# Outputs' tiles in their own pool over the stored rows, the first unit filled like the later ones, and a finished half's projection at earlier places

## The chip, the cores and the metric

The kernel runs on one core of one Trainium2 chip. The metric is device time in microseconds (us) of one launch; lower is better. TensorE is called PE, VectorE DVE, ScalarE ACT, GpSimd POOL and SyncE SP, as in the profile.

## The reference

A model of two layers on x of shape (B=2, T=1024, E=256), all in float32. Every block is followed by a residual add and a layernorm over E.

```python
x = layernorm(x + attn0(x))   # causal grouped-query attention: 32 q heads, 8 kv heads, D=8, rope, softmax
x = layernorm(x + ffn0(x))    # silu(x Wg * sg) * (x Wu * su), then Wd * sd; int8 weights, FF=1024
x = layernorm(x + attn1(x))   # gated delta rule, below
x = layernorm(x + ffn1(x))    # relu(x sign(Wu)^T * s) sign(Wd)^T * s, FF=1024

# attn1: 16 heads, key and value width 128
q, k, v = silu(conv4(x Wq)), silu(conv4(x Wk)), silu(conv4(x Wv))   # causal depthwise conv over 4 tokens
a, b = sigmoid(x Wa + ba), sigmoid(x Wb + bb)                       # per token and head
for t:                                                              # per batch and head; k scaled by 128**-0.5
    S = a_t * S - b_t * (S k_t - v_t) k_t^T
    o_t = S q_t
o = layernorm_per_head(o) * ln_w + ln_b
return (o * sigmoid(x Wg)) Wo
```

## The kernel before

Products that need float32 accuracy are split in a high and a low part and done as three matmuls each (`mm3`, L968 to L970).

**Order.** Layer 0 (attention, then FFN in blocks of two token tiles of 128, 16 tiles in all) ends at about 803 us of the span. Then comes the delta rule (`delta_rule`), as 32 *units*. `place(i)` gives unit i as (hi, s): hi is one of four halves of 512 tokens, s one of eight pairs of heads. A unit has two heads and four chunks of 128 tokens. So units 7, 15, 23 and 31 (s == NS - 1) are the last ones of a half: with them a half's rows are complete.

PE's order in the delta rule is written by hand: each piece of work is a generator that yields the place of its next step, each unit has 120 places (`UNIT`), and `lines.add(generator, at, base)` puts it in. On PE instructions keep this order strictly (`te.link`, `te.strict`). On the other engines and on SP's queue of DMA issues the framework's scheduler decides the order, and each engine then works its queue in order.

Pieces of a unit i:

- `recur(i)`, the chain over four chunks c: `pr` (place 30c; L673 and L677, transposed v plus k times the state M), copied by ACT to `prs` (L680); `pw` (30c+10, L688), copied to `wc` (L691); then `pm` (L700) and `po` (L715, L716) at 30c+20. DVE makes the next state M (L705 from no state, L707 else), ACT copies po to `o` (L719), DVE takes its moments (`ost`, `om`, L657, L658).
- `others(i+1)`: v projection of the next unit (place 1), q (31), key rows, gate (61), gate rows, scores `pkq` (71, 81). The projections' convolutions are four taps (L275) on DVE, `far` and `halos` (L289, L272) on ACT, adds (L292) on POOL.
- `keys(i+4)` (AHEAD = 4): k projection at AT_KEYS = 91, decay scans (L325) on DVE at 113, triangles (L339) from 131.
- `decayed`: POOL multiplies k and q by the decay rows `dg` (L519, L521), which a DMA on SP's queue loads.
- `blocks` (even i; a chain of small DVE steps on `pi` and `tmp`, L384 and L390) and `levels` (odd i; L420 `p`, L423 `n` on DVE, L431 `px`), which build the inverse of the triangles.
- `finish(i)`, which runs inside unit i+1 at the four places AT_FINISH: normalises o with a reciprocal root `om` (`rsqrt`: L931 to L933 on DVE, then twelve small steps on POOL, L940 to L943, then L599 on DVE; the eight tiles of o are then normalised by POOL, DVE and ACT in turn, L606 and L609), transposes it (`pt`, L615, two heads at the first two places), multiplies with the gate `gt` (`y`, L619), splits y in `yh` and `yl` (POOL, L623 and L917), and at the last two places projects with Wo (`pf`, 12 matmuls each, L633) and adds to the residual rows `xtok` (L636). For s == NS - 1 a layernorm of these rows follows each of the two adds: bn statistics (L948, L949), `rsqrt` on DVE (L931 to L938, on the tile `ln`), scaling (L952). After both, the half is stored (`store_tokens`, L927).

Before unit 0, `rest_of_first` sets up what the first unit needs: decays and decayed k, q of unit 0, then the v and q projections of unit 1, and the k projection and convolution of unit 4. In later units these stand inside the unit before.

**Pools.** At the start of the delta rule the SBUF of layer 0's rows (`x`, pool `toks`) and of its FFN is free again. `open_late` opens over it one pool ("late") for the tiles of the recurrence (prs, wc, M, o, om, ost) and of the output (gt, xtok, wo, y, yh, yl), and one ("w") for weights and decay rows.

**Layer 0's last steps.** Each FFN block ends with `layernorm(..., eng=nc.gpsimd)` on two token tiles (three rounds of a root step: twelve steps on POOL, or nine on DVE where `eng` is None) and a store of those rows. The last block's layernorm runs while unit 1's projections have begun.

The line numbers are those of the kernel before.

Of the kernel before, what the change touches and what calls it, by code (L numbers as in the profile page):

```python
# [12 lines left out]
F32R = mybir.dt.float32r  # L13
# [7 lines left out]
P = 128  # L21
# [10 lines left out]
HP = 2  # L32
# [56 lines left out]
AT_LEVELS = 43, 53, 73, 83, 103, 113, 132, 142  # L89
AT_FFN = 24  # L90
AT_FINISH, AT_FINISH_LAST, AT_HALF = (41, 51, 101, 111), (31, 41, 71, 76), ((22, 30, 46), (1, 6, 13))

FFN0, FFN1, FFN1_LAST, FFN1_TAIL = 7.6, 22.0, 27.0, 40.0

# [50 lines left out]
def delta_rule(  # L145
# [23 lines left out]
    ps_m = open_pool(left, "ps_m", "left", 2, PSUM)  # L169

    def open_late():
        pools["late"] = open_pool(right, "dlate", "right", 2)
        pools["w"] = open_pool(outer, "dw", "right")
        for name, bufs in (("c", 2), ("t", 1), ("l", 1)):
            pools[name] = open_pool(right, "ps_" + name, "right", bufs, PSUM)
# [6 lines left out]
    def half_tile(pool, tag, bufs):  # L182
        return pool.tile([P, HT], F32, name=tag, tag=tag, bufs=bufs)
# [297 lines left out]
    def pair(m, i):  # L481

        pps = [project(m, i, h) for h in range(HP)]
        for h in range(HP):
            conv(m, i, h, pps[h])
        if i < last:
            yield AT_OUT
        for h in range(HP):
            conv_out(m, i, h, pps[h])
# [35 lines left out]

    def gate_rows(i):
        for h in range(HP):
            g = half_tile(pools["late"], "gt", 5)
            made = nc.scalar.activation(g, st[i]["pg"][h], AF.Tanh, scale=0.5)
            if copied:  # L530
                after(made, copied[-1])
            st[i]["gt", h] = g
# [25 lines left out]
    def rest_of_first():  # L558
        decays(0)
        for which in "kq":  # L560
            for h in range(HP):
                decayed(0, h, which)
        te.strict, te.last = True, ended[0]
        for m in "vq":
            drain(pair(m, 1))
        ks = keys(AHEAD, AT_KEYS)
        next(ks)
        lines.add(ks, next(ks), 0)

    def gate_of_first():  # L570
        gate(0)
        yield GAP
        gate_rows(0)

    def finish(i, o, m, chunks, places):

        hi, s = place(i)
        if s == 0:
            halves[hi]["x"] = load_tokens(pools["late"], hi * HC, HC)
        x = halves[hi]["x"]  # L580
        if chunks[0] == 0:
            st[i]["wo"] = []
            for part in range(2):
                t = pools["late"].tile([P, HP, E], F32R, name=f"wo{part}", tag=f"wo{part}", bufs=1)
                nc.sync.dma_start(
                    out=t.bitcast(F32),
                    in_=w1d["o", part][s * HP * P : (s + 1) * HP * P, :].rearrange("(h p) e -> p h e", p=P),
                )
                st[i]["wo"].append(t)
        wo = st[i]["wo"]  # L590
        c1, nc_ = chunks[0], len(chunks)
        final = i == last and chunks[-1] == HC - 1
        slow = None if i == last else nc.gpsimd
        ahead = tc.high_priority if final else nullcontext
        t1 = slice(c1 * P, (c1 + nc_) * P)
        rs, nb = m[:, :, 2], m[:, :, 3]
        with ahead():
            rsqrt(rs, m[:, :, 1], m[:, :, 4], m[:, :, 5], EPS * SCALE * SCALE, slow)
            nc.vector.scalar_tensor_tensor(nb, m[:, :, 0], -1.0, rs, ALU.mult, ALU.mult)  # L599
            for c in chunks:  # L600
                for h in range(HP):
                    n = (c - c1) * HP + h
                    oc, r1 = o[:, c, h, :], rs[:, n : n + 1]
                    how = (NORM if i < last else NORM_LAST)[n]
                    if how == "A":
                        nc.scalar.activation(oc, oc, AF.Identity, bias=nb[:, n : n + 1], scale=r1)  # L606
                    else:
                        eng = nc.gpsimd if how == "P" else nc.vector
                        eng.tensor_scalar(oc, oc, m[:, n, 0:1], r1, ALU.subtract, ALU.mult)  # L609
        ys = []  # L610
        for h in range(HP):
            yield places[h]
            pt = bank(pools["t"], "t", "pt")[:, 0 : nc_ * P]
            for c in chunks:
                te.link(nc.tensor.transpose(pt[:, (c - c1) * P : (c - c1 + 1) * P], o[:, c, h, :], ident))  # L615
            y = half_tile(pools["late"], "y", 1)[:, 0 : nc_ * P]
            with tc.high_priority():
                nc.scalar.activation(pt, pt, AF.Identity, bias=lnb, scale=lnw)
                nc.vector.scalar_tensor_tensor(y, st[i]["gt", h][:, t1], 1.0, pt, ALU.add, ALU.mult)  # L619
            yh = pools["late"].tile([P, HT], F32R, name="yh", tag="yh", bufs=2)[:, 0 : nc_ * P]  # L620
            yl = pools["late"].tile([P, HT], F32R, name="yl", tag="yl", bufs=2)[:, 0 : nc_ * P]
            with ahead():
                (nc.gpsimd.tensor_copy if i < last else nc.scalar.copy)(yh, y)  # L623
                sub_low(nc.gpsimd if i < last else nc.vector, yl, y, yh)
            ys.append((yh, yl))
        for c0 in range(0, nc_, 2):
            yield places[2 + c0 // 2]
            pf = bank(pools["t"], "t", "pf").rearrange("p (c e) -> p c e", e=E)
            for c in range(2):
                for h in range(HP):  # L630
                    t = slice((c0 + c) * P, (c0 + c + 1) * P)
                    yh, yl = ys[h]
                    mm3(pf[:, c, :], yh[:, t], yl[:, t], wo[0][:, h, :], wo[1][:, h, :], h == 0, h == HP - 1)  # L633
            xc = x[:, c1 + c0 : c1 + c0 + 2, :]
            with ahead():
                nc.vector.tensor_add(xc, pf, xc)  # L636
                if s == NS - 1:
                    layernorm(gx, x, c1 + c0, 2, eng=nc.gpsimd if i == last and not final else None)
            if s == NS - 1:
                halves[hi]["done"] = c1 + c0 + 2  # L640
        if s == NS - 1 and hi < 2 * B - 1:
            store_tokens(xs, hi * HC, x)

    def recur(i):
# [8 lines left out]
        def moments(c):  # L653
            for h in range(HP):
                st6 = pools["late"].tile([P, 6], F32, name="ost", tag="ost")
                with tc.high_priority() if i == last and c == HC - 1 else nullcontext():
                    nc.vector.bn_stats(st6, o[:, c, h, :])  # L657
                    nc.vector.bn_aggr(m[:, c * HP + h, 0:2], st6)  # L658
            part = HC // 2 if i == last else HC
            if c % part == part - 1:  # L660
                chunks = range(c + 1 - part, c + 1)
                at = i * UNIT + 3 * GAP * (c + 1) + 3
                lines.add(finish(
                    i, o, m[:, chunks[0] * HP : (c + 1) * HP, :], chunks,
                    AT_HALF[c // part] if i == last else AT_FINISH_LAST if i == last - 1 else AT_FINISH,
                ), at, at if i == last else (i + 1) * UNIT)

        for c in range(HC):
# [172 lines left out]
    def drain(g):  # L841
        for _ in g:
            pass

    for i in range(-AHEAD, last + 1):
# [9 lines left out]
            open_late()  # L855
        if i < -1:
            lines.add(keys(i + AHEAD, 0), t)
        elif i > 0 and i + AHEAD <= last:
            lines.add(keys(i + AHEAD, AT_KEYS), t + AT_KEYS, t)
        if i == -2:  # L860
            lines.add(others(0), t)
# [3 lines left out]
        elif 0 <= i < last:  # L865
            lines.add(others(i + 1), t + AT_ROWS, t)
        if i == 0:
            lines.add(gate_of_first(), t + AT_QUERIES)
        if i >= 0:
            lines.add(recur(i), t, chain=True)  # L870
# [27 lines left out]
def tile_two_layers(ctx: ExitStack, tc: tile.TileContext, a, out):  # L898
# [22 lines left out]
    def load_tokens(pool, n, count, bufs=1, tag="xtok"):  # L921
        t = pool.tile([P, count, E], F32, name="xtok", tag=tag, bufs=bufs)
        nc.sync.dma_start(out=t, in_=xs[n * P : (n + count) * P, :].rearrange("(n p) e -> p n e", p=P))
        return t
# [91 lines left out]
    def open_pool(group, name, side, bufs=1, space=bass.MemoryType.SB):  # L1016
        return group.enter_context(tc.tile_pool(name=name, bufs=bufs, side=side, space=space))
# [467 lines left out]
    def open_ffn(group):  # L1485
# [20 lines left out]
        def block(n):  # L1506
# [45 lines left out]
            with tc.high_priority() if n == NT - 2 else nullcontext():  # L1552
                for i in range(2):
                    y = new("fy", [P, E], 2)
                    nc.vector.tensor_mul(y, po[i], s_down)
                    nc.vector.tensor_add(x[:, n + i, :], y, x[:, n + i, :])
                anchor["norm"] = layernorm(pool, x, n, 2, eng=nc.gpsimd)
                store_tokens(xs, n, x[:, n : n + 2, :])
            yield 0.2

# [127 lines left out]
```

## Time and profile before

| | |
|---|---|
| median of 3 runs | 2052.26 us (2052.05 to 2056.88) |
| profiled execution | 2052.92 us, of it span 2051.20 us, 1.72 us around it |
| mean granted TensorE clock | 0.977 |
| PE busy | 1888.1 us |
| DVE, ACT, POOL busy | 1475.0, 1266.7, 1077.4 us |
| delta rule, from the first prs copy | at 821.0 us of the span |
| units 0, 1, 2, 3 (from prs to prs) | 26.2, 37.1, 31.3, 38.9 us |
| units 8, 9; 16, 17; 24, 25 | 33.5, 43.4; 30.9, 49.7; 33.5, 40.1 us |
| PE idle within units 9, 17, 25 | 5.6, 9.5, 3.5 us |

Busy PE time is time with a matmul on the array; the granted clock is the share of full speed at which it ran. The length of a unit is the time between the first copies (prs, L680) of two successive units. Even units of a batch's first half have less to do than odd units, which also carry `levels`; units are therefore compared with others of the same parity. In an answer of waits a row reads: engine and line, what it waited for, us in total, times, longest.

### The profile page before, as it was taken

The numbers are of one execution on the slowest core, as the hardware profiler recorded it, in microseconds if no ns is written. First come the engines' busy times: TensorE is split into PE (matmuls) and PEld (weight loads), VectorE is DVE, ScalarE is ACT, GpSimd is POOL, SyncE is SP. The second block draws the span as 40 slices with busy tenths as digits, with TensorE's granted clock in tenths as the row PEclk, the third lists the DMA queues.
The fourth block names the chain that finished last, engine by engine and source line by source line (L and its number), as shares of the span: only waits on it lengthen the run. The fifth ranks groups of instructions, "written<-read, shape, count | busy, mean of one in ns | idle before, by whom it ended". The sixth has DMA issues, their size and how long they took to land.

```text
span 2051.2 us, 49222 instructions
## 1 busy us (share of the span) xinstructions
PE 1888.1 (92%) x18657; PEld 1491.8 (73%) x18657; DVE 1475.0 (72%) x3477; ACT 1266.7 (62%) x2731; POOL 1077.4 (53%) x1739
## 2 busy tenths in 40 slices
PE   5898889999998898999999899999899999999986
PEld 3454455555556787888889789888888888888775
DVE  5756666887756995676787787678678679766566
ACT  1365556566655366567676676776676766676542
POOL 4353333331124464666776656666567676665453
PEclk8999999999999999899999999999999999999997
DMA  5564443441232431443444434345434344443010
GB/s 169 165 190 133 147 131 125 149 135 55 69 77 62 116 92 55 134 123 110 127 115 116 142 99 118 115 115 137 116 101 133 114 126 109 125 135 96 18 52 22
DMA packets 312998, 229.17 MB, mean 112 GB/s; under 512 B 139640, under 2 KB 278904, under 8 KB 312760
## 3 DMA queue, kind: packets, MB, share of 16 engines
q1 hardware_dynamic: 299640, 210.73, 35.3%
q10 hardware_dynamic: 9760, 10.83, 1.6%
q0 software_dynamic: 3360, 4.46, 0.9%
q8 instruction: 147, 2.41, 0.5%
q14 instruction: 91, 0.75, 0.1%
HBM read 171.18 MB, written 51.87 MB: 109 GB/s over the span
## 4 chain that ended last, share of the span: by engine, by line
PE 57%; DVE 11%; DMA 6%; ACT 5%; POOL 4%; issue 3%; SPq 1%; DVEq 0%; ACTq 0%; POOLq 0%
PE pp L968 5%; PE pp L969 4%; PE pp L970 4%; PE ps L1342 4%; PE av L1363 4%; PE ps L1273 3%; PE pkq L508 3%; PE pm L700 2%; PE pr L677 2%; DVE at L325 2%; PE pw L688 2%; PE po L716 2%; PE po L715 2%; PE p L478 2%; PE p L471 2%
## 5 line engine op out<-in xcount | busy, mean ns | idle before, releaser
L1282 DVE TENSOR_REDUCE mx<-ps 128x4 f32<-128x1024 f32 (+1 forms) x320 | 344.2, 1111 | 130.1 <-PE ps L1273 89.3
L1346 ACT ACTIVATE es<-ps 128x512 f32<-128x512 f32 (+1 forms) x608 | 313.9, 578 | 127.2 <-PE ps L1342 116.7
L1342 PE MATMUL ps<-qT,kT 128*128 128x512 f32 (+3 forms) x768 | 219.1, 368 | 19.2 <-ACT es L1346 18.4
L1273 PE MATMUL ps<-kT,qT 128*128 128x512 f32 x576 | 200.0, 421 | 28.1 <-DVE mx L1282 18.1
L1342 PEld LDWEIGHTS ps<-qT,kT 128*128 128x128 f32 x768 | 129.6, 188 | 105.2 <-ACT es L1346 59.6
L1273 PEld LDWEIGHTS ps<-kT,qT 128*128 128x128 f32 x576 | 101.8, 191 | 88.7 <-DVE mx L1282 48.0
L289 ACT ACTIVATE far<-pp,cw 128x509 f32<-128x509 f32 x192 | 133.2, 699 | 46.6 <-DVE k L275 18.8
L1363 PE MATMUL av<-es,vaug 128*32 128x512 f32 (+3 forms) x1536 | 156.7, 496 | 0.7 <-POOL es L1349 0.7
L917 POOL TENSOR_TENSOR wfl<-wf,wfh 128x256 fp32r<-128x256 f32 x80 | 58.4, 733 | 187.2 <-ACT wfh L1006 155.9
L1349 POOL TENSOR_SCALAR_AFFINE_SELECT es<-es 128x512 f32<-128x512 f32 x128 | 80.2, 635 | 145.3 <-ACT es L1346 141.7
L275 DVE SCALAR_TENSOR_TENSOR q<-pp,cw,q 128x511 f32<-128x511 f32 (+1 forms) x128 | 93.2, 742 | 47.6 <-ACT halos L272 24.2
L275 DVE SCALAR_TENSOR_TENSOR k<-pp,cw,k 128x511 f32<-128x511 f32 (+1 forms) x128 | 92.1, 743 | 45.5 <-ACT k L268 25.0
L292 POOL TENSOR_TENSOR q<-q,far 128x509 f32<-128x509 f32 x64 | 69.3, 1085 | 97.8 <-ACT far L289 97.7
L275 DVE SCALAR_TENSOR_TENSOR v<-pp,cw,v 128x511 f32<-128x511 f32 (+1 forms) x128 | 92.2, 739 | 33.4 <-ACT v L268 18.3
L292 POOL TENSOR_TENSOR k<-k,far 128x509 f32<-128x509 f32 x64 | 77.7, 1215 | 51.2 <-ACT far L289 50.6
L519 POOL TENSOR_TENSOR k<-k,dg 128x508 f32<-128x508 f32 x64 | 82.2, 1284 | 33.0 <-PE pkq L508 29.0
L1006 ACT CAST wfh<-wf 128x256 fp32r<-128x256 f32 x80 | 32.3, 405 | 107.4 <-DMA wf<-in_w1k 35.7
L716 PE MATMUL po<-wc,at 128*128 128x128 f32 x512 | 96.8, 276 | 0.0
L680 ACT COPY prs<-pr 128x256 f32<-128x256 f32 x128 | 48.8, 381 | 77.7 <-PE pr L677 69.5
L325 DVE TENSOR_TENSOR_SCAN at<-da,d 128x512 f32<-128x512 f32 x64 | 90.1, 1448 | 0.0
L700 PE MATMUL pm<-wc,kc 128*128 128x128 f32 x448 | 77.6, 296 | 11.4 <-ACT wc L691 11.4
L688 PEld LDWEIGHTS pw<-prs,lt 128*128 128x128 f32 x512 | 76.7, 191 | 14.9 <-ACT prs L680 3.0
(323 smaller groups left out, 5916.2 us busy)
## 6 DMA issues: line engine op xcount, KB each, us to landing
wk<-w1k SPq DMA_DIRECT2D x64, 256.0 KB
da<-dec SPq DMA_DIRECT2D x64, 256.0 KB
wv<-w1v SPq DMA_DIRECT2D x64, 256.0 KB
wq<-w1q SPq DMA_DIRECT2D x64, 256.0 KB
dg<-dec SPq DMA_DIRECT2D x64, 256.0 KB
wg<-w1g SPq DMA_DIRECT2D x64, 256.0 KB
wo<-w1o SPq DMA_DIRECT2D x64, 256.0 KB
ad<-avs ACTq DMA_DIRECT2D x32, 256.0 KB
```

Source lines behind the costliest of these rows:

```text
L275: made = nc.vector.scalar_tensor_tensor(acc[:, d:], pp[:, 0 : HT - d], cw[:, n, hd, KS - 1 - d : KS - d], acc[:, d:], ALU.mult, ALU.add)
L289: made = nc.scalar.activation(far[:, w], pp[:, w], AF.Copy, scale=cw[:, n, hd, 0:1])
L292: nc.gpsimd.tensor_add(acc[:, KS - 1 :], acc[:, KS - 1 :], far[:, w])
L325: nc.vector.tensor_tensor_scan(e, dec, d1.rearrange("p c t -> p (c t)"), 0.0, ALU.mult, ALU.add), taps
L688: te.link(nc.tensor.matmul(pw[:, r], lhsT=lt[:, h * HC + c, :], rhs=prs[:, r], start=True, stop=True))
L700: te.link(nc.tensor.matmul(pm[:, r], lhsT=st[i]["kc", h][:, c, :], rhs=wc[:, r], start=True, stop=True))
L716: te.link(nc.tensor.matmul(po[:, r], lhsT=st[i]["at", h][:, t], rhs=wc[:, r], start=(M is None), stop=True))
L1273: anchor["mm"] = te.link(nc.tensor.matmul(ps[:, j - j0, :].rearrange("p (g k) -> p g k", k=P), lhsT=q_, rhs=kT[:, :, j * P : (j + 1) * P], ...
L1282: nc.vector.tensor_reduce(mx[:, it, j0 // 2, :], ps[:, 0:n, :].rearrange("p j (g k) -> p g j k", k=P), AX.XY, ALU.max)
L1342: te.link(nc.tensor.matmul(ps[:, g - g0, :], lhsT=kT[:, g, jb * P : (jb + 1) * P], rhs=qT[:, i0 : i0 + w], start=True, stop=True,))
L1346: exps.append(nc.scalar.activation(es[:, g0 : g0 + n, 0:w], ps, AF.Exp, scale=D ** -0.5))
L1363: mm = te.link(nc.tensor.matmul(av[ROW * g : ROW * (g + 1), i0 - ih * 512 : 512], lhsT=vaugs[b][:, jb, kv, :], rhs=es[:, g, 0:w], start=(j ...
```

## The change

1. A new pool ("out", `dout`), opened ahead of "late", takes gt, xtok, wo, y, yh and yl; it lies where the stored rows x lay. The other tiles stay in "late".
2. `rest_of_first` drains the v projection of unit 1 only. The q projection of unit 1 is put into unit 0 at place 1 (`first_queries`), and the keys of unit 4 come into unit 0 at AT_KEYS, as in all later units.
3. Units that end a half (s == NS - 1, except the last) use the places 41, 51, 86, 94 for `finish` in the next unit instead of 41, 51, 101, 111: the projection and the residual add come earlier.
4. The last FFN block of layer 0 does its reciprocal root on DVE (nine steps) instead of POOL (twelve).

The number of instructions on PE, ACT and SP stays; POOL has 12 fewer, DVE 8 more.

```diff
+AT_FINISH_ROWS = 41, 51, 86, 94
...
     def open_late():
+        pools["out"] = open_pool(right, "dout", "right", 2)
         pools["late"] = open_pool(right, "dlate", "right", 2)
         pools["w"] = open_pool(outer, "dw", "right")
...
     def gate_rows(i):
         for h in range(HP):
-            g = half_tile(pools["late"], "gt", 5)
+            g = half_tile(pools["out"], "gt", 5)
...
         te.strict, te.last = True, ended[0]
-        for m in "vq":
-            drain(pair(m, 1))
-        ks = keys(AHEAD, AT_KEYS)
-        next(ks)
-        lines.add(ks, next(ks), 0)
+        drain(pair("v", 1))
+
+    def first_queries():
+        for _ in pair("q", 1):
+            yield AT_ROWS + AT_OUT
...
     def finish(i, o, m, chunks, places):
...
-            halves[hi]["x"] = load_tokens(pools["late"], hi * HC, HC)
+            halves[hi]["x"] = load_tokens(pools["out"], hi * HC, HC)
...
-                t = pools["late"].tile([P, HP, E], F32R, name=f"wo{part}", tag=f"wo{part}", bufs=1)
+                t = pools["out"].tile([P, HP, E], F32R, name=f"wo{part}", tag=f"wo{part}", bufs=1)
...
-            y = half_tile(pools["late"], "y", 1)[:, 0 : nc_ * P]
+            y = half_tile(pools["out"], "y", 1)[:, 0 : nc_ * P]
...
-            yh = pools["late"].tile([P, HT], F32R, name="yh", tag="yh", bufs=2)[:, 0 : nc_ * P]
-            yl = pools["late"].tile([P, HT], F32R, name="yl", tag="yl", bufs=2)[:, 0 : nc_ * P]
+            yh = pools["out"].tile([P, HT], F32R, name="yh", tag="yh", bufs=2)[:, 0 : nc_ * P]
+            yl = pools["out"].tile([P, HT], F32R, name="yl", tag="yl", bufs=2)[:, 0 : nc_ * P]
...
-                    AT_HALF[c // part] if i == last else AT_FINISH_LAST if i == last - 1 else AT_FINISH,
+                    AT_HALF[c // part] if i == last else AT_FINISH_LAST if i == last - 1
+                    else AT_FINISH_ROWS if s == NS - 1 else AT_FINISH,
...
         if i < -1:
             lines.add(keys(i + AHEAD, 0), t)
-        elif i > 0 and i + AHEAD <= last:
+        elif i >= 0 and i + AHEAD <= last:
             lines.add(keys(i + AHEAD, AT_KEYS), t + AT_KEYS, t)
...
         if i == 0:
+            lines.add(first_queries(), t + AT_ROWS)
             lines.add(gate_of_first(), t + AT_QUERIES)
...
-                anchor["norm"] = layernorm(pool, x, n, 2, eng=nc.gpsimd)
+                anchor["norm"] = layernorm(pool, x, n, 2, eng=nc.gpsimd if n < NT - 2 else None)
```

## The prediction

> **What bounds the kernel now.** I read the page first, then the chain, then tables of busy time by stretch around the places the change touches, then PE's waits and the rows of the timeline there.
>
> From the page of before, busy times, the clock slices and the chain by engine:
> ```profile
> PE 1888.1 (92%) x18657; PEld 1491.8 (73%) x18657; DVE 1475.0 (72%) x3477; ACT 1266.7 (62%) x2731; POOL 1077.4 (53%) x1739
> PEclk8999999999999999899999999999999999999997
> PE 57%; DVE 11%; DMA 6%; ACT 5%; POOL 4%; issue 3%; SPq 1%; DVEq 0%; ACTq 0%; POOLq 0%
> ```
> PE is the bound of the whole, so time is lost only where PE stands idle or runs at a lower clock. The change adds and removes no matmul, so it can act only on these two. The clock slices show one dip outside the ends, the 9 to 8 in the middle (slice 17, about 820 to 870 us): the passage from layer 0 to layer 1, which the change rewrites.
>
> Busy time by stretch (columns: PE, PEld, DVE, ACT, POOL, granted clock, DMA share, GB/s), first the passage, then the starts of units 9 and 17:
> ```profile
> 800.00:820.00 20.00, 13.41 (x44) 9.70 (x45) 13.17 (x36) 10.37 (x22) 8.34 (x19) 0.79 0.32 100
> 820.00:840.00 20.00, 17.32 (x83) 14.34 (x82) 11.03 (x35) 8.60 (x25) 10.58 (x10) 0.70 0.69 203
> 1130.00:1150.00 20.00, 16.04 (x349) 13.99 (x349) 20.00 (x75) 15.04 (x33) 12.44 (x24) 1.00 0.44 119
> 1435.00:1440.00 5.00, 0.00 (x0) 0.00 (x0) 4.96 (x17) 2.27 (x4) 3.38 (x8) 0.61 0.26 86
> 1440.00:1445.00 5.00, 3.80 (x116) 2.87 (x120) 1.89 (x6) 2.77 (x7) 2.83 (x4) 0.50 0.38 122
> ```
> The passage loses about 9 us of PE and some 10 us of clock (40 x 0.255), part of it not to be had. In unit 9 DVE is full for 20 us of 20 while PE idles 4: there the wait that ends last is DVE's. In unit 17 PE does nothing for 5 us and then works at half clock: idle time costs twice.
>
> Who ends PE's waits, in the passage, unit 9 and unit 17:
> ```profile
> PE pp L968 <- ACT far L289: 5.8, 3, 2.1
> PE px L431 <- DVE n L423: 2.3, 1, 2.3
> PE pt L615 <- POOL o L609: 7.7, 2, 7.1
> ```
> The last one is the chain that decides below: o is normalised with a reciprocal root `om`, made by DVE up to L933, then by twelve POOL steps (L940-943), then L599 and L609, and only then PE may transpose (L615). Its place in DVE's queue in unit 9, beside the layernorm `ln` of the finished half:
> ```profile
> 1124.32 0.68 DVE L636 TENSOR_TENSOR xtok<-pf,xtok 128x512 f32<-128x512 f32 x1
> 1133.13 0.17 DVE L933 TENSOR_SCALAR om<-om 128x8 int32<-128x8 int32 x1
> 1140.36 1.02 DVE L938 SCALAR_TENSOR_TENSOR ln<-ln 128x2 f32<-128x2 f32 x1
> 1137.83 2.48 POOL L609 TENSOR_SCALAR o<-o,om 128x128 f32<-128x128 f32 x3
> 1139.98 0.71 PE L615 MATMUL pt<-ident,o 128*128 128x128 f32 x4
> 1147.05 1.58 PE L431 MATMUL px<-n,dt 32*32 32x32 f32 x128 [2.26 <-DVE n L423]
> ```
> L933 to the first transpose: 6.85 us; from there to px 7.07 us, of which 2.26 idle.
>
> **The pool.** gt, xtok, wo, y, yh and yl get a pool of their own, other tiles keep theirs. No instruction is added. What it can move is only when the first of these tiles may be written over the stored rows of layer 0. The built program has SP's 1374 issues as before, in another order at the start of layer 1. 0 us, bounds -1 to +1 (the 0.92 and 0.81 us single waits of the passage are the nearest rows).
>
> **The first unit.** Taken off the path ahead of unit 0: the q pair of unit 1 (12 matmuls, 808.36 to 811.5 after a wait of 1.82) and the k pair of unit 4 (813.45 to 820.04 with waits of 1.92 and 2.11 and half clock). They come back inside unit 0: q at place 1, k at place 91. The new order on PE is v, pr, q, then pw. The first pr needs nothing of the two pairs, so its copy prs, at 821.0 before, can stand at about 812.5, and pw of the first chunk at 812.9. But unit 0 then stops at something else. The decays of k and q on POOL (L519, L521, 1.26 and 1.27 us) wait for the rows dg, whose load stands in SP's queue right behind the store of layer 0's last rows (xs, L927, issued at 815.83): issued at 816.29, landed at 820.9. M of the first chunk is free early (about 816.5 instead of 826.65, since two DVE scans of 4.02 us no longer stand ahead), but pr of the second chunk waits for the second head's decayed k.
>
> **The last layernorm of layer 0.** Its twelve POOL steps (809.42 to 813.64, two v adds of 1.08 between) become nine DVE steps. A serial step on DVE takes 0.20 us (rows of the last layernorm of the kernel, L936 to L938, start to start), 9 x 0.20 = 1.8, and DVE idles 1.99 us at that place (the row of L275 at 811.08 waits for ACT). So xs is stored about 2.2 us earlier, at 813.6, and dg lands at about 818.4 (4.6 us from issue to landing, plus the issue). If that idle time were not there, the 1.8 us would fall on the q taps, whose adds end after dg anyway. What is late next: POOL's first decay ends at 819.9, the second k at 823.5 behind a q add of 1.08. PE idles in part from 815 to 823.5, does gate(0) at half clock (5 us, as before) and pw of chunk 1 at about 828.6 instead of 832.75: 4.1 us earlier. From there it still owes the k pair, 12 matmuls at 0.235 = 2.8 us. Unit 1 would start 1.3 us earlier (2.2 with the clock back sooner). Against that, unit 1 gets the filling of later odd units: from its last pw to the next prs 34.6 us before, 36.3 in unit 3, +1.7. Sum of the passage: about 0. From both sides: -5 (half of the 10 us of idle saved) and +3 (k and the taps of unit 0 collide with the decays).
>
> **Projection at 86 and 94.** It concerns finish of units 7, 15 and 23, that is units 8/9, 16/17 and 24/25. The 2 x 12 matmuls of pf (1.4 us each half) move ahead of unit 8's third pw; its SP loads stay. The first half must wait for yl (POOL, to 1120.27): about 1 us of stall, and that pw moves from 1121.98 to about 1126. DVE is full from 1110 to 1150, so an earlier layernorm gives nothing by itself; it only changes who stands first. The order of the built program: the first add L636, its bn statistics and all nine root steps in one run now stand ahead of the k taps, and om's L933 stands after both adds, the scaling L952 and three v taps.
>
> Unit 9, DVE from the last pi at 1122.3 up to om's L933, start-to-start times of the rows of before: two adds 1.2, four k taps 2.7, two scans 3.1, bn of ln 1.3, two L952 1.3, bn of o 0.4, k ends 0.8, three v taps 2.0, one triangle and M 1.1, transpose 0.6, thirteen serial small steps 2.6, ten small ones in gaps 0.7 = 17.8, so 1140.1 instead of 1133.13. With 6.85 to the transpose and 7.07 - 2.26 = 4.8 of PE work to px: 1140.1 + 6.85 + 4.8 = 1151.8 instead of 1147.05: +4.7. The idle time is now over 5 us in one piece; unit 17 paid 10.24 us of half clock after 7.1, so one step of 3.41 us at half, 1.7. One small DVE step that meets a POOL add takes 1.0 instead of 0.15 (the L938 row above; at 1435.63 another takes 0.99): one such in the serial run, +0.85. Unit 9: +7.3, bounds 0 (DVE does the same sum of work) and +10.
>
> The Trainium skill, "SBUF — State Buffer", Who interferes with whom, states that a VectorE instruction with two SBUF inputs and a GpSimd instruction that reads SBUF exclude each other for the whole instruction. It speaks against root steps on VectorE where POOL adds: by it, each of the two 1.08 us v adds could hold the nine steps in the passage once, and the rows would be stored 2 us later, so at the old time; by the 1.99 us idle row alone they come 2.2 earlier.
>
> Unit 25: the same new order; PE idles 3.52 in it before: +4.7 + 0.85 = +5.5, bounds 0 to +8.
>
> Unit 17 is odd in that before `om` came very late. DVE from 1415.8: adds 1.2, k taps 2.7, scans 2.9, bn 1.3, M 0.5, bn of o 0.4, L952 1.4, one v tap 0.7, six serial steps 1.2, small ones 1.1 = 13.4, so L933 at 1429.2 instead of 1432.54. Then 3.5 us of POOL steps and a v add of 1.08; but M's copy L705 now stands behind three v taps, so pr of chunk 1 and the q pair come 3 us later, and pw at 1436. First transpose at about 1437, not 1440.63, and the second wait (0.57) goes: -4.3, and one of three half-clock steps, -1.7: -6.0, bounds -11 to -2.
>
> **Sum.** 0 + 7.3 + 5.5 - 6.0 = +6.8. The profiled execution took 2052.92 us (span 2051.20, 1.72 around it), 0.66 over the median of 2052.26, so I add to the median and round: 2059.0.
>
> **Rivals.**
> *Faster: unit 17's stall goes and units 9 and 25 hold.* One mechanism: with the half's layernorm run off early, POOL's om steps of unit 17 start so soon that the transpose waits for PE alone: its 9.54 us of idle fall to the 1.7 of units 13 or 21, -7.8, and two of three half-clock steps go, -3.4; if in 9 and 25 om's extra wait is covered by the q pair, they cost 0. With -0.8 from the passage: 2052.3 - 12 = 2040. For it: that stall is the longest of the boundaries and its releaser is POOL. Against: L705 moves back there. It decides if the first transpose of unit 9 is at most 1 us later than before.
> *No change: DVE's sum decides.* Units 9 and 25 are full on DVE and the order inside does not count (0 and 0), unit 17's gain is eaten by L705 (-2), passage +1: 2051. For it: 20.00 of 20.00. Against: a queue in order puts om where it stands. The variant that the change does not do what it says (SBUF addresses of the new pool still wait for the old rows) costs no more than 1 us and ends here too.
>
> **Chances.** Units 9 and 25 pushed back 0.55 (own range 2055 to 2067), faster 0.25, no change 0.20. A measurement of this kernel can tell about 0.3%, 6.2 us, from no change. Of the first case 0.44 lies above 2058.4, 0.11 below; of the second 0.24 below 2046.1, with 0.01 within; of the third 0.14 within, 0.03 to each side. That makes 0.27 faster, 0.26 same, 0.47 slower. The range takes the middle of the second case and the bounds of the first: 2039 to 2067.
>
> **What would show it.** Right: in unit 9 the first L615 at about 1147 counted in the old clock, after a wait for POOL's L609, and the same in unit 25; in unit 17 the 7.1 us wait shrinks to 3 or 4 and a new wait of about 3 us for M L705 stands in front of its second pr; the first pw at 813, and dg landing near 818. Wrong: a wait of the second pr for dg well past 824 (the passage then costs), or L615 in unit 9 where it was (the second rival), or half-clock stretches that vanish after 1436 (the first).

## The result, and the profile after

The changed kernel takes 2066.94 us (median of 11 runs, 2057.40 to 2068.62) against 2053.57 us (11 runs, 2049.31 to 2058.21) of the kernel before on the same chip: a ratio of 1.0056, 95% interval 1.0044 to 1.0067, so about 11.5 us slower (the medians alone lie 13.4 us apart). The forecast was slower, +6.8 us with a range of 2039 to 2067: the measured time stands at the upper edge of that range, which also holds the time of the kernel before.

The profiled execution has a span of 2065.17 us, 14.0 more than that of before. To see where, both traces are cut at events that both have: the last matmul of layer 0 (L1546 before, L1552 after), and the first copies prs of units. All values in us:

| stretch | before | after | difference | forecast |
|---|---|---|---|---|
| start to layer 0's last matmul | 802.5 | 807.6 | +5.1 | 0 |
| from there to unit 0's first prs | 18.5 | 11.9 | -6.6 | -8.5 |
| unit 0 | 26.2 | 33.3 | +7.1 | +7 |
| unit 1 | 37.1 | 40.3 | +3.2 | +1.7 |
| units 2 to 7 | 211.6 | 211.7 | +0.1 | 0 |
| units 8, 9 | 76.9 | 82.3 | +5.4 | +7.3 |
| units 10 to 15 | 217.3 | 217.2 | -0.1 | 0 |
| units 16, 17 | 80.5 | 75.7 | -4.8 | -6.0 |
| units 18 to 23 | 218.6 | 216.7 | -1.9 | 0 |
| units 24, 25 | 73.7 | 81.0 | +7.3 | +5.5 |
| unit 26 to the end | 288.4 | 287.5 | -0.9 | 0 |

The first row is not the change: up to there all engines have the same instructions in the same order. Over the 14 traces of this study, whose programs are all alike up to there, layer 0 ends between 801.7 and 808.2 us. So spans of two executions cannot be compared to better than 6 us, and the text below compares stretches instead. The four rows that the change touches (passage with units 0 and 1; 8, 9; 16, 17; 24, 25) give +3.6, +5.4, -4.8 and +7.3, in sum +11.5.

From the page of after, the rows that answer to those of before:
```profile
PE 1896.0 (92%) x18657; PEld 1494.8 (72%) x18657; DVE 1474.7 (71%) x3486; ACT 1268.3 (61%) x2731; POOL 1074.1 (52%) x1727
PEclk9999999999999899999999999999999999999997
PE 56%; DVE 12%; ACT 5%; DMA 5%; POOL 4%; issue 3%; SPq 1%; DVEq 0%; ACTq 0%; POOLq 0%
```
They look almost the same. A loss of half a per cent is not to be read from this page. It shows the 12 POOL steps less and nine DVE steps more (3486 against 3477; the section on the change says eight).

Busy time by stretch of after, the passage first, then unit 9 from its start on, then unit 17 where PE had been empty:
```profile
805.00:825.00 20.00, 12.56 (x49) 8.99 (x49) 15.63 (x50) 9.56 (x21) 5.31 (x7) 0.83 0.35 115
825.00:845.00 20.00, 15.93 (x82) 13.26 (x83) 6.19 (x28) 6.59 (x19) 6.92 (x6) 0.74 0.54 156
1140.40:1160.40 20.00, 13.02 (x148) 10.73 (x152) 17.50 (x54) 12.85 (x26) 13.22 (x25) 0.89 0.45 138
1450.00:1455.00 5.00, 4.37 (x151) 3.60 (x150) 4.90 (x15) 3.04 (x7) 2.51 (x4) 1.00 0.59 169
```
The passage did not get denser: PE does 28.5 of 40 us instead of 30.7. In unit 9 PE now idles 7 of 20 us, and half clock has moved into this stretch. Unit 17 is mended: PE works, at full clock.

Who ends PE's waits in after, in the order passage, units 8/9, 16/17 and 24/25:
```profile
PE pr L682 <- POOL k L522: 5.8, 2, 3.3
PE pt L619 <- POOL o L613: 4.4, 2, 3.9
PE pr L682 <- DVE M L710: 2.0, 1, 2.0
PE pt L619 <- POOL o L613: 3.3, 1, 3.3
```
(L682 is before's L677, L619 its L615, L613 its L609, L710 its L705.) The long wait for POOL's o has left unit 17 and sits in units 9 and 25; in unit 17 the new wait for M's copy stands where it was expected.

The timeline of after around unit 9's start, the same steps as shown of before (unit 8 starts 8.9 us later here):
```profile
1131.11 0.68 DVE L640 TENSOR_TENSOR xtok<-pf,xtok 128x512 f32<-128x512 f32 x1
1149.31 0.85 DVE L939 TENSOR_SCALAR om<-om 128x8 int32<-128x8 int32 x1
1155.53 2.48 POOL L613 TENSOR_SCALAR o<-o,om 128x128 f32<-128x128 f32 x3
1156.47 1.01 PE L619 MATMUL pt<-ident,o 128*128 128x128 f32 x3 [3.86 <-POOL o L613]
1164.40 1.62 PE L434 MATMUL px<-n,dt 32*32 32x32 f32 x128
```
The first add comes 2 us earlier in this count, om's third step (L939, before's L933) 7.3 us later, the first transpose 7.6 later, px 8.4 later.

The passage in after (POOL, DVE, ACT, PE):
```profile
813.76 1.08 POOL L295 TENSOR_TENSOR v<-v,far 128x509 f32<-128x509 f32 x1 [6.43 <-ACT far L292]
813.80 1.07 DVE L939 TENSOR_SCALAR ln<-ln 128x2 int32<-128x2 int32 x1
816.42 1.01 DVE L944 SCALAR_TENSOR_TENSOR ln<-ln 128x2 f32<-128x2 f32 x1
818.68 0.15 ACT L275 COPY halos<-pp 128x3 f32<-128x3 f32 x1
819.48 0.37 ACT L685 COPY prs<-pr 128x256 f32<-128x256 f32 x1 [0.65 <-DVE x L958]
824.99 1.26 POOL L522 TENSOR_TENSOR k<-k,dg 128x508 f32<-128x508 f32 x1 [2.21 <-DMA dg<-dec]
826.30 0.80 PE L682 MATMUL pr<-M,k 128*128 128x128 f32 x2 [3.32 <-POOL k L522]
```
Two small steps of the root take 1.0 us instead of 0.16, each while POOL adds v (the second add ran from 816.32 to 817.40). The first copy prs stands on ACT behind steps that end at 818.83 and then waits 0.65 us for the end of that layernorm (L958, 819.45); pr of the second chunk waits for k, multiplied with dg.

### The profile page after: what moved, and what is told of

It reads as the page before. It is cut to its first block, busy times and chain, and to the rows that moved or that the text cites. A ratio compares the mean times of both kernels' runs of the same rounds, so it can differ in the third digit from the quotient of the medians.

```text
span 2065.2 us, 49210 instructions
## 1 busy us (share of the span) xinstructions
PE 1896.0 (92%) x18657; PEld 1494.8 (72%) x18657; DVE 1474.7 (71%) x3486; ACT 1268.3 (61%) x2731; POOL 1074.1 (52%) x1727
## 4 chain that ended last, share of the span: by engine, by line
PE 56%; DVE 12%; ACT 5%; DMA 5%; POOL 4%; issue 3%; SPq 1%; DVEq 0%; ACTq 0%; POOLq 0%
PE pp L974 5%; PE pp L976 4%; PE pp L975 4%; PE ps L1348 4%; PE av L1369 4%; PE ps L1279 3%; PE pkq L511 3%; PE pm L705 2%; PE pw L693 2%; DVE at L328 2%; PE po L721 2%; PE pr L682 2%; PE po L720 2%; PE p L481 2%; PE p L474 2%
## 5 line engine op out<-in xcount | busy, mean ns | idle before, releaser
L1355 POOL TENSOR_SCALAR_AFFINE_SELECT es<-es 128x512 f32<-128x512 f32 x128 | 80.3, 635 | 146.9 <-ACT es L1352 140.2
L278 DVE SCALAR_TENSOR_TENSOR k<-pp,cw,k 128x511 f32<-128x511 f32 (+1 forms) x128 | 92.2, 744 | 46.2 <-ACT k L271 24.1
L295 POOL TENSOR_TENSOR k<-k,far 128x509 f32<-128x509 f32 x64 | 76.5, 1196 | 48.2 <-ACT far L292 47.6
L1012 ACT CAST wfh<-wf 128x256 fp32r<-128x256 f32 x80 | 32.3, 405 | 104.2 <-DMA wf<-in_w1k 33.3
L682 PE MATMUL pr<-M,k 128*128 128x128 f32 x448 | 82.4, 279 | 11.4 <-POOL k L522 5.8
L705 PE MATMUL pm<-wc,kc 128*128 128x128 f32 x448 | 77.9, 297 | 13.6 <-ACT wc L696 13.5
L1369 PEld LDWEIGHTS av<-es,vaug 128*32 128x32 f32 x1536 | 39.0, 110 | 67.9 <-issue 50.7
```

The lines of the kernel that those rows point to most:

```text
L278: made = nc.vector.scalar_tensor_tensor(acc[:, d:], pp[:, 0 : HT - d], cw[:, n, hd, KS - 1 - d : KS - d], acc[:, d:], ALU.mult, ALU.add)
L295: nc.gpsimd.tensor_add(acc[:, KS - 1 :], acc[:, KS - 1 :], far[:, w])
L682: te.link(nc.tensor.matmul(pr[:, r], lhsT=st[i]["k", h][:, t], rhs=M[:, r], start=False, stop=True))
L705: te.link(nc.tensor.matmul(pm[:, r], lhsT=st[i]["kc", h][:, c, :], rhs=wc[:, r], start=True, stop=True))
L1369: mm = te.link(nc.tensor.matmul(av[ROW * g : ROW * (g + 1), i0 - ih * 512 : 512], lhsT=vaugs[b][:, jb, kv, :], rhs=es[:, g, 0:w], start=(j ...
```

## The experiments

Theory A is that of the prediction: the loss sits at the starts of units 9 and 25, because the layernorm of a finished half moves ahead of om and n in DVE's queue; the places themselves and the pool cost nothing. Theory B puts the loss into the passage, theory C into PE's own order (pf earlier, pw later). Each run has 5 rounds beside the kernel before; a ratio is to the runs of before on the same chip. Times of stretches are from one trace of each kernel (how well they repeat is told behind run 12); P, F, N and R stand for the pool, the first unit's filling, the root on DVE and the new places.

| kernel | parts | ratio (95%) | passage and units 0, 1 | 8, 9 | 16, 17 | 24, 25 |
|---|---|---|---|---|---|---|
| before | | | 81.9 | 76.9 | 80.5 | 73.7 |
| changed | P F N R | 1.0056 (1.0044 to 1.0067) | 85.5 | 82.3 | 75.7 | 81.0 |
| 1 | P F N | 1.0005 (0.9990 to 1.0021) | 84.3 | 72.7 | 80.2 | 72.8 |
| 2 | R | 0.9987 (0.9978 to 0.9996) | 82.5 | 76.3 | 76.3 | 75.7 |
| 3 | F | 1.0008 (0.9997 to 1.0019) | 83.6 | 76.8 | 80.9 | 73.7 |
| 4 | R in unit 15 | 0.9974 (0.9962 to 0.9985) | 83.3 | 75.4 | 75.4 | 73.8 |
| 5 | P F N R, om first | 0.9999 (0.9986 to 1.0012) | 86.6 | 78.9 | 73.6 | 76.7 |
| 6 | P N R | 1.0013 (1.0001 to 1.0025) | 83.0 | 76.1 | 76.8 | 83.2 |
| 7 | N, R in unit 15 | 0.9951 (0.9932 to 0.9970) | 82.6 | 73.1 | 76.6 | 72.9 |
| 8 | N | 0.9972 (0.9955 to 0.9989) | 82.4 | 72.1 | 80.9 | 73.1 |
| 9 | P F N, R in unit 15 | 0.9962 (0.9948 to 0.9975) | 84.5 | 72.3 | 76.2 | 72.4 |
| 10 | P | 1.0004 (0.9992 to 1.0015) | 83.8 | 75.9 | 80.3 | 73.8 |
| 11 | N, R and om first in unit 15 | 0.9929 (0.9913 to 0.9945) | 82.3 | 72.1 | 73.6 | 72.8 |
| 12 | P F N R, dg first | 1.0022 (1.0006 to 1.0038) | 82.2 | 75.3 | 76.4 | 83.3 |

**1. The new places undone.**
```diff
-                    else AT_FINISH_ROWS if s == NS - 1 else AT_FINISH,
+                    else AT_FINISH,
```


> The changed kernel, with a finished half's projection back at the places 101 and 111. Theory A (the order of DVE's queue at the starts of units 9, 17 and 25 makes most of the loss): units 8/9, 16/17 and 24/25 become as long as before (76.9, 80.5, 73.7 us), and about 8 us of the loss go; what is left of the change is the passage from layer 0, +3 to +4 us, ratio to before 1.000 to 1.003. Theory B (the loss is the passage, and the 5 us by which layer 0 ended later in the profiled execution belong to the change): +8 to +9 us stay, ratio 1.004 or more, and layer 0's last matmul stands near 807 us again.

Ratio 1.0005. The loss at 24/25 goes and unit 17's stall returns, as theory A says. Units 8/9 do more: 72.7, four under before. In the built program the scheduler puts n (L423) and the next state M (L707) ahead of the half's scaling (L952) there, which is the order that the kernel before has in unit 25. n stands 15.4 us after unit 9's start instead of 16.9, and the half-clock step that unit 9 had (3.41 us) does not come. Run 3 shows that n alone does not do it: there n stands at 15.6, but M behind two scalings, and 8/9 take 76.8. Theory B falls: the loss that stays is the passage, +2.4. The four stretches together give -3.0 us in this trace, the ratio +1.0 (-2.1 to +4.3), so sums of stretches of single traces are not better than a few microseconds.

**2. The new places alone.**
```diff
+AT_FINISH_ROWS = 41, 51, 86, 94
...
+                    else AT_FINISH_ROWS if s == NS - 1 else AT_FINISH,
```


> The kernel before, with the places 86 and 94 for a finished half's projection and nothing else of the change. Theory A: +5 us in units 8 and 9, -5 in 16 and 17, +7 in 24 and 25: about +8 us, ratio near 1.004. Theory B: within 2 us of before, ratio 1.000 to 1.001. Layer 0 is the same program as before, so its end (802 us in the profile of before) shows how much it moves by itself.

A miss for theory A's +8: ratio 0.9987, a gain. Unit 17 gains 4.2 as in the changed kernel, but 8/9 stay (76.3) and 24/25 lose 2.0 only. The places alone are therefore not the cause. The waits of unit 9 of this kernel:
```profile
PE pt L616 <- POOL o L610: 0.9, 1, 0.9
PE pt L616 <- ACT o L607: 0.8, 1, 0.8
```
and its timeline:
```profile
1140.59 0.16 DVE L935 TENSOR_SCALAR om<-om 128x8 int32<-128x8 int32 x1
1146.24 0.17 DVE L600 SCALAR_TENSOR_TENSOR om<-om 128x8 f32<-128x8 f32 x1
1146.29 0.33 PE L616 MATMUL pt<-ident,o 128*128 128x128 f32 x1 [0.90 <-POOL o L610]
```
Unit 9 starts at 1132.80 here, so om's third step is at +7.8 and the first transpose at +13.5; before it was +3.7 and +10.5, after +8.9 and +16.0. Three microseconds later, the transpose cost nothing here: PE stands idle for 4.9 us in units 8 and 9, before 5.7. The order on DVE differs between this kernel and the changed one: here four of the nine root steps and the first scaling stand behind the k taps. The same places gave two orders in DVE's queue, since the scheduler orders DVE anew for each program.

**3. The first unit's filling alone.**
```diff
-        for m in "vq":
-            drain(pair(m, 1))
-        ks = keys(AHEAD, AT_KEYS)
-        next(ks)
-        lines.add(ks, next(ks), 0)
+        drain(pair("v", 1))
...
+            lines.add(first_queries(), t + AT_ROWS)
```


> The kernel before, with the first unit filled as the later ones (q of unit 1 and keys of unit 4 inside unit 0) and nothing else. Theory A: from the end of layer 0 to the start of unit 2 it takes 0 to +4 us more than before (82.1), since PE now waits for the decayed k instead of doing the two projections; ratio 1.000 to 1.002. Theory B: +4 us or more in this stretch, with the pool and the root on DVE giving nothing back.

+1.7 in the passage with units 0 and 1, ratio 1.0008: a small loss or none. Over the traces with it (changed, 1, 3, 5, 9; run 12, which also moves dg, is left out) the stretch takes 84.9 on average, over the eight without (before, 2, 4, 6, 7, 8, 10, 11) 82.7: +2.2. All of it is unit 1, 40.3 against 37.6; the way to unit 1's start is half a microsecond shorter.

**4. The new places for unit 15 alone.**
```diff
+                    else AT_FINISH_ROWS if i == 15 else AT_FINISH,
```


> The kernel before, with the places 86 and 94 for unit 15 alone, so only units 16 and 17 change. Theory A: 16 and 17 together fall from 80.5 to about 75.7 us and nothing else moves: -4 to -5 us, ratio near 0.998. If instead what one boundary gains is handed back at the next (units 18 to 25 longer), the ratio is 1.000.

16/17 fall by 5.1, ratio 0.9974; nothing is handed back later. 8/9 are 1.5 shorter than before with the same order on DVE.

**5. Order forced on DVE: the layernorm behind om.**
```diff
+        if s == NS - 1 and i < last:
+            for c0 in range(0, nc_, 2):
+                yield (126, 127)[c0 // 2]
+                layernorm(gx, x, c1 + c0, 2, hold=st[i + 1]["om"])   # its first root step after om's third
```


> The changed kernel with one order forced: pf and its add stay at 86 and 94, but the root of the finished half's layernorm may start on DVE only behind L933 of the next o normalisation (om). Theory A (om's place in DVE's queue sets PE's wait in units 9 and 25): 8/9 fall from 82.3 to 72-76 us and 24/25 from 81.0 to 72-76 us, 16/17 stay at 74-77; in all 10 us or more under the changed kernel, ratio to before 0.997 to 1.000. Theory C (the earlier pf on PE, its wait for yl and the later pw, is what costs): 8/9 and 24/25 stay above 80 us, ratio 1.005.

PE's order is that of the changed kernel (apart from some 32x32 matmuls that start within 0.01 us of each other), pf at 86 and 94 with its wait for yl too. 8/9 fall by 3.4 us, 24/25 by 4.3, 16/17 by 2.1, and the ratio from 1.0056 to 0.9999. So theory C does not carry the loss, and om's place does carry most of it. But 78.9 and 76.7 are above the 72 to 76 expected. The waits of units 8 and 9 show why:
```profile
PE px L434 <- DVE n L426: 2.3, 1, 2.3
PE pt L619 <- POOL o L613: 1.1, 1, 1.1
PE pf L984 <- POOL yl L928: 1.0, 1, 1.0
```
The transpose's wait is down from 4.4 to 1.1, but now n stands behind all four scalings of the half and px waits 2.3 for it. Two steps on DVE matter there, om and n. In unit 25 the order and these waits are the same; that its pair is 2.2 us shorter goes with the clock, 6.83 us at half clock in unit 9 and none in unit 25.

**6. The changed kernel with the first unit as before.**
```diff
-        drain(pair("v", 1))
+        for m in "vq":
+            drain(pair(m, 1))
+        ks = keys(AHEAD, AT_KEYS)
```


> The changed kernel with the first unit as before (pool, root on DVE and the new places stay). In the built program DVE's order in unit 9 is that of the run with the places alone (8/9 took 76.3 us there), in unit 25 one with om later still. Theory A: 8/9 at 75-77 us, 24/25 between 75 and 81, 16/17 at 75-77; the end of layer 0 to the start of unit 2 back at 81-83 us; ratio to before 0.998 to 1.001. If the first unit's filling had nothing to do with units 8 and 9, they stay at 82 us.

8/9 at 76.1 as its order said, the ratio 1.0013 just above its range; 24/25 at 83.2, two over the range, with this wait for the transposes in units 24 and 25:
```profile
PE pt L618 <- POOL o L612: 5.5, 2, 4.3
```
The passage is back at 83.0.

**7. Root on DVE, and the places for unit 15.**
```diff
-                anchor["norm"] = layernorm(pool, x, n, 2, eng=nc.gpsimd)
+                anchor["norm"] = layernorm(pool, x, n, 2, eng=nc.gpsimd if n < NT - 2 else None)
...
+                    else AT_FINISH_ROWS if i == 15 else AT_FINISH,
```


> The kernel before, with the root of layer 0's last layernorm on DVE and the new places for unit 15 alone. In the built program DVE's order in unit 9 puts n (L423) ahead of the scaling (L952), as in the changed kernel without the new places (8/9 took 72.7 us there). Theory A: 8/9 at 72-74, 16/17 at 75-77, 24/25 at 73-74 us; 8 to 9 us under before, ratio 0.995 to 0.997, the fastest so far. Without the gain of units 8 and 9 the ratio is 0.9975 as with unit 15's places alone.

As theory A expected, to 0.1 us in each stretch; ratio 0.9951.

**8. Root on DVE alone.**
```diff
+                anchor["norm"] = layernorm(pool, x, n, 2, eng=nc.gpsimd if n < NT - 2 else None)
```


> The kernel before, with the root of layer 0's last layernorm on DVE and nothing else. Theory A: in the passage the rows dg land up to 2 us earlier, but M and ACT's far set PE there, so 0 to -2 us from the end of layer 0 to the start of unit 2; units 8/9 at 72-74 us instead of 76.9 because the scheduler's order there turns with it: ratio 0.997 to 0.999. Rival: nine steps in DVE's queue between the taps delay them, +1 to +2 us in the passage.

The passage does not move (82.4 against 82.7 on average without the filling), but 8/9 fall to 72.1, because the order of DVE 300 us later turns with it. In its own place the root does what the prediction said: counted from layer 0's last matmul, xs is stored 2.8 us earlier than before (10.6 against 13.4) and the first decayed k starts 2.5 earlier (16.0 against 18.4), but PE gains nothing from it. An edit that yields nothing in its own place gives a ratio of 0.9972.

**9. The changed kernel with the places for unit 15 alone.**
```diff
-                    else AT_FINISH_ROWS if s == NS - 1 else AT_FINISH,
+                    else AT_FINISH_ROWS if i == 15 else AT_FINISH,
```


> The changed kernel with the new places for unit 15 alone; pool, first unit and root on DVE stay. Theory A: 8/9 at 72-74 us, 16/17 at 75-77, 24/25 at 72-74, against 82.3, 75.7 and 81.0 in the changed kernel; the end of layer 0 to the start of unit 2 stays at 84-86 us: ratio to before 0.996 to 0.999. If the first unit's filling or the pool were the cause, 8/9 stay above 80 us and the ratio above 1.004.

Every stretch as theory A said, ratio 0.9962: the change as a whole is a gain once units 7 and 23 keep the old places.

**10. The pool alone.**
```diff
+        pools["out"] = open_pool(right, "dout", "right", 2)
```


> The kernel before, with the pool of the outputs' tiles and nothing else. DVE's order in units 9, 17 and 25 of the built program is that of before. Theory A: every part as before within a microsecond (8/9 at 76-77, 16/17 at 80-81, 24/25 at 73-74 us, the passage at 81-83), ratio 0.999 to 1.001. Rival: another release of the memory under the new pool makes the passage 2 us longer or shorter.

No effect that these runs can tell, 1.0004 (0.9992 to 1.0015). Its passage is 83.8, above the 81 to 83 expected and the longest without the filling, where the others spread from 81.9 to 83.3. The next longest is run 4, which has no pool. In these two traces a whole half-clock step of 3.41 us lies behind layer 0's last matmul and the fourth v tap starts 7.2 us after it; in the other six it is 3.0 us at most, and the tap starts after 4.9 to 6.2. So the trace gives no reason to charge the pool, though a loss of half a microsecond is not excluded.

**11. The best of these.** Kernel 7, and for unit 15 the hold of kernel 5.
```diff
+        if i == 15:
+            for c0 in range(0, nc_, 2):
+                yield (126, 127)[c0 // 2]
+                layernorm(gx, x, c1 + c0, 2, hold=st[i + 1]["om"])
```


> The kernel before, with the root of layer 0's last layernorm on DVE, and for unit 15 alone the new places and the half's layernorm held behind om in DVE's queue (as in the run with om first). Theory A: 8/9 at 72-74, 16/17 at 73-75, 24/25 at 72-74 us: 10 to 12 us under before, ratio 0.993 to 0.996, 2 to 3 us under the run without the hold. If DVE's sum of work decides and not its order, 16/17 stay at 76-77 us.

2042.02 us median, ratio 0.9929 (0.9913 to 0.9945), the fastest. 16/17 fall by another 3.0 us; PE no longer waits for o in unit 17:
```profile
PE pr L684 <- DVE M L712: 1.1, 1, 1.1
PE px L432 <- DVE n L424: 0.2, 1, 0.2
```

**12. The whole change, with dg's loads first.**
```diff
-        decays(0)
+        with tc.high_priority():
+            decays(0)
```


> The whole changed kernel, with the two loads of the decay rows dg of unit 0 put ahead of the last store of xs in SP's queue. In the built program this also turns DVE's order in unit 9 into that of the run with the places alone (76.3 us), and in unit 25 into that of the run with the first unit as before (83.2 us). Theory A: 8/9 at 75-77 us instead of 82.3, 24/25 at 81-84 us; dg lands no more than 1 us earlier after layer 0's end if the load waits for memory that the last layernorm still uses, and 4 us or more earlier if SP's order was what held it; ratio to before 1.001 to 1.004. If the parts themselves and not the order count, 8/9 stay at 82 us.

This is the sharpest pair: all four parts, PE's order that of the changed kernel (as in run 5), and in unit 9 another order on DVE, by a side effect of an edit 300 us earlier. 8/9 take 75.3 us instead of 82.3: PE stands idle for 5.2 us in them instead of 8.6, and the 6.83 us at half clock are gone. In 24/25 the scheduler chose an even later om, 83.3. The waits of the transposes in units 9 and 25:
```profile
PE pt L620 <- POOL o L614: 0.9, 1, 0.9
PE pt L620 <- POOL o L614: 5.4, 2, 4.3
```
Some steps of ACT and POOL move there together with those of DVE; no run holds them and moves DVE's alone, so that DVE's place leads is read from the chain om, POOL's steps, transpose. dg is issued 11.3 us after layer 0's end instead of 12.3, 0.06 us behind the end of the last layernorm, which itself ends 0.6 earlier here; the first decayed k starts at 15.7 instead of 17.4. That is nearer to the 1 us expected of a wait for memory than to the 4 us of a wait in SP's queue alone. The passage with units 0 and 1 shortens by 3.3, about 1.7 of it by one half-clock step less.

**The same order, the same length.** The traces can be sorted by DVE's order around the odd unit's start (times of om's third step, the first transpose and n after that start; numbers of the runs in brackets):

| order | om, transpose, n | 8/9 | 24/25 |
|---|---|---|---|
| before's in unit 25 | 3.7, 10.5, 15.4 | 72.1 to 73.1 (1, 7, 8, 9, 11) | 72.4 to 73.8 (before, 1, 3, 4, 7 to 11) |
| before's in unit 9 | 3.7, 10.5, 16.9 | 75.4 to 76.9 (before, 4, 10) | |
| run 3's | 3.7, 10.5, 15.6 | 76.8 (3) | |
| om first | 5.2, 12.0, 20.0 | 78.9 (5) | 76.7 (5) |
| of the places alone | 7.8, 13.5, 18.8 | 75.3 to 76.3 (2, 6, 12) | 75.7 (2) |
| changed kernel's | 8.9, 16.0, 20.9; in 25 9.3, 16.6, 21.7 | 82.3 | 81.0 |
| om last | 13.2, 18.9, 24.1 | | 83.2, 83.3 (6, 12) |

The length goes with the order, whichever parts of the change brought it, and one order repeats to within 2.2 us.

## Why the prediction was right, point by point

- **What bounds.** Right: PE has the same work, and the losses are waits and half clock at places where another engine ends last.
- **The sum, +6.8.** Right in sign and mechanism, too small by 4.7: the passage is 3.6 over its term, unit 25 1.8, unit 17 1.2, unit 9 1.9 under. That the errors partly cancel is luck.
- **The pool, 0.** Right within what can be told of it alone (run 10).
- **The first copy prs.** Wrong: the prediction had it at 812.5 because its inputs are ready then; it came at 819.5, which is 814.3 when layer 0's end is laid on that of before (5.1 earlier), and the first pw at 814.8 instead of 813. On ACT it stands behind the v and q steps up to 818.83, and the last 0.65 us are put down to the last layernorm's L958. In run 3, with the first unit's filling but without the pool and the root on DVE, ACT stands idle for it and it comes 14.6 us after layer 0's end instead of 11.9; the wait is put down to a step of pi on DVE:
```profile
819.35 0.37 ACT L682 COPY prs<-pr 128x256 f32<-128x256 f32 x1 [4.65 <-DVE pi L391]
```
A wait of prs for DVE stood in no sum. That it is one for memory which prs may not write yet is likely, since pi is no input of prs, but no run shows it. Of the 2.7 us nothing is left at the start of unit 1 (43.4 us after layer 0's end in run 3, 45.2 in the changed kernel).
- **The root on DVE.** Right in size, though less in this trace. The prediction put the nine steps into an idle stretch of 1.99 us at 0.20 us each and had xs 2.2 and the first decayed k 2.5 us earlier; alone (run 8) they gave 2.8 and 2.5, and the averages of the runs with and without it (run 12 left out) differ by 2.4 and 2.2. In the trace of the changed kernel xs was stored 1.5 us earlier (11.9 against 13.4 us after layer 0's end) and k came 1.1 earlier (17.4 against 18.4). There the third and fourth v taps start 0.4 and 1.3 us later after layer 0's end than before, with a whole half-clock step behind it as in runs 4 and 10; the nine steps come behind the fourth tap (815.5), and one of them met a POOL add. The page of the Trainium skill named there, "SBUF — State Buffer", Who interferes with whom, says that a VectorE instruction with two SBUF inputs and a GpSimd instruction that reads SBUF exclude each other. The row of 1.01 us (L944, two inputs) beside a 1.08 us add agrees with it. The row of 1.07 us is of a step with one input (L939), for which that sentence says nothing; its step on om in unit 9 took 0.85 us beside an add too.
- **The first unit, 0.** Mis-sized: +2.2 on average over the runs, +3.6 for the whole passage in the trace shown. The way to unit 1's start came out as a draw (forecast -1.3 to -2.2); the second head's k was at 828.5, five less counted as before, as late as foreseen. The term for unit 1's own filling was +1.7 and measured +2.7 (the 34.6 and 36.3 us behind that term run from the unit's first pw to the next prs, not from its last).
- **Unit 9, +7.3.** Its steps hold: om +7.0 forecast, +7.3 measured; first transpose +7.0 and +7.6; px +4.7 and +8.4. The waits grew as said, the half clock went from 3.41 to 6.83 us. The later part of the unit gave back 3 us, so +5.4: behind px the kernel before had an idle time of 1.59 us and its half-clock step, the changed one has neither.
- **Unit 25, +5.5.** +7.3. Counted from unit 24's start the first transpose comes 6.5 us later, after a wait of 3.3 for POOL's o, as foreseen. PE's idle time in both units grew by 3.7 us, less than the sum had; three steps of half clock (10.24 us) were not in that sum, which took none.
- **Unit 17, -6.0.** -4.8. Counted from unit 16's start the first transpose came 4.0 us earlier (3.6 in the working, which with the 0.57 makes 4.2 and not 4.3), the new wait for M took 2.0 (3 foreseen), all half clock went.
- **The rivals.** The second, that DVE's sum decides and not its order, falls with runs 5 and 12, where the same work in another order takes 3.4 and 7.0 us less in 8/9. The first, that units 9 and 25 hold, did not come here, but it comes with another order of the same parts (units 8/9 in runs 6 and 12). The prediction took the order from the built program, and that is why its sign held: by the places alone (run 2) it would have been a gain.

What is not settled: why the scheduler's choice in units 9 and 25 turns with edits far ahead is not known; and the cost of the first unit's filling within unit 1 (2.7 us, of it 2.2 us of idle PE in the trace) has no run of its own.

## What to carry to other kernels

Where an engine is full for 20 us, the time of an edit is decided by who stands first in its queue, and a scheduler decides that anew for each program: read the order of the built kernel before costing an edit, and pin the one or two steps that the bottleneck waits for. Compare stretches between the same events in both traces, not spans. When a change of several parts loses, try each part, and each place of a part: here one of three places carried the gain and the other two the loss.

## What the runs showed of the hardware that was not expected

- Layer 0, the same program in all 14 traces, took 801.7 to 808.2 us. The traces of before and after differ there in half-clock time, 35.4 against 41.0 us, and in the waits. Over all 14 the half-clock time does not explain it: run 10 ends layer 0 last, at 808.2 with 37.5 us of it, run 12 at 806.8 with 48.2. The cause stays open.
- Half clock comes in steps of 3.41 us. "TensorE: Matmul & The Clock Gate", What's actually happening, states that the clock is halved after an idle window of about 3.4 us; the steps agree, the condition does not quite: in unit 9 of before the longest idle time of PE was 2.26 us, and a step of 3.41 us at half clock followed 12 us later, behind an idle time of 1.59. In run 1, where the idle times of this unit were 1.37 and 0.77 us, there was none. Runs 4 and 10 have the order of before there, and the step came 1.5 us behind the idle time of 2.26. One idle time can bring two steps or three: behind the 7.1 us of unit 17 half clock lasted 10.24 us before and in runs 3 and 8, 6.83 in runs 1 and 10.
- A DVE step on 2 values per partition (0.16 us) can take 1.07 us when it meets a POOL add of 1.08 us, with one input (L939) as well as with two (L944).
